# Layers 1 to 3 of a four-layer graph attention kernel: program order instead of a scheduler's order, earlier weight loads, later stores

## The chip, the cores and the metric

The kernel runs on one core of a Trainium2 chip. The metric is the device time of one execution in microseconds (us), lower is better. The kernel before takes 2342.57 us (median of three runs, 2339.33 to 2343.09).

## What is computed

Four graph attention layers in a row over 4096 nodes with 256 features each, all with the same adjacency matrix (about one entry in 256 set, and the diagonal). Each layer projects the features, makes a score for every pair of neighbours out of a term of the row and a term of the column, takes the softmax over the neighbours of a row, sums the neighbours' values with these weights, adds the layer's input and normalises the row. Cut to its core (h is the projection, a1 and a2 are the attention vectors):

```python
s1, s2 = h @ a1, h @ a2
e = leaky_relu(s1[:, None] + s2[None, :], 0.2)
e = where(adj > 0, e, -inf)
x = layernorm(x + softmax(e) @ h)
```

Layers 0 and 1 have four heads of 64 features, layer 2 two heads of 128 with biases. Layer 3 has one score, but two softmaxes (of e and of -e) over the unprojected x, a product with a matrix for both, and an ELU. All arithmetic is in float32.

## The kernel before

The adjacency matrix is sparse, so a row tile (128 rows) doesn't meet all 4096 columns. While layer 0 runs, `lists` packs the columns that each row tile needs into 13 groups of 128 column indices (`idx`) and a mask for each group (`maskC`). With the row tile's own 128 columns there are 14 positions, in two halves of seven.

**A row tile** (class `RowTile`). `load` brings the edge terms S (L619), the mask mk (L621), the tile's own value rows G (L626, "own-row load") and the input rows y (L925) through SyncE's queue, and 13 gathers of value rows by index through GpSimd (L629). `half` makes the weights of seven positions: in layers 1 and 2 ScalarE's exponentials L670 with VectorE's masked products L671, in layer 1 also VectorE's L666 and L667; in layer 3 ScalarE's L657, L658 and L660 with VectorE's L659 and L661. TensorE multiplies weights and values (L679 in layer 1, L682 in layers 2 and 3). In layer 1 ScalarE copies the sum out (L689) and TensorE transposes it back (L697). `finish` divides by the softmax's sum and adds y (L982, L983, L985; in layer 3 L967, L970 and L987 to L995), and `norm` normalises the row on VectorE: L935, L936, and then 15 operations on one number for each row (L944 to L954), among them three Newton steps for an inverse square root, each step of four operations that need one another's results, and L956, which writes y. L958 stores y.

**A projection** (class `Projection`) follows for each finished row tile of layers 0 to 2: transpose (L532), copy (L537 on ScalarE), product (L546, L549), row (L564 to L572, stored by L574), edge (L578, L584, stored by L585). Its results are what the next layer gathers.

**Whole rows** (`whole_rows`). In layer 2 the last twelve row tiles, in layer 3 the last four, are not gathered: four row tiles at a time meet all 32 column tiles in turn (`units`), with values loaded by L888, a mask by L886 and edge terms once for a block of four, ScalarE's L900 (in layer 3 L903 with L905 or L907), VectorE's L901 (L908) and TensorE's L911. `whole` advances the units between the halves of the gathered row tiles. When a block's last unit is done, `whole_rows` calls `finish` for its four rows, one after the other.

**Buffers.** S and mk have 4 buffers, w 10, G 16 slots (and 14 more for the second halves in layer 3), pw 8, vw 6, y 9.

**What sets the order.** The kernel is written as a software pipeline: `part` runs twice for each row tile m, loads what m and m+1 still lack, and then `half_alone` (layers 0, 1) or `half_with_whole` (layers 2, 3) issues one half with pieces of the projection and of the finish of m-1; `close` joins a layer to the next. But this order isn't the one on the engines. The framework's scheduler [...] puts each engine's instructions in the order of that plan. An engine runs its queue in that order, and so does SyncE with the loads and stores: an entry that waits holds what is behind it.

The weights of the next layer are made in row tile 2 by `weights`: loads of a few matrices and vectors, small products on TensorE (L270, L279) and their scaling (L258 to L262).

Of the kernel before, what the change touches and what calls it, by code (L numbers as in the profile page):

```python
# [37 lines left out]
F32 = mybir.dt.float32  # L38
# [12 lines left out]
P = 128  # L51
# [78 lines left out]
def to_tiles(ap):  # L130
    return ap.rearrange("(t p) f -> p t f", p=P)
# [55 lines left out]
class Program:  # L187
# [24 lines left out]

    def weights(self, n):

        nc, ins, H = self.nc, self.ins, HEADS[n]
        V = F if n < 3 else 2 * F
        wext = self.wpool.tile([P, KT, 2 * F + 4 * H4], F32, name="wext")
        ablks, nats, brow = [], [], None
        if n < 2:
            nc.sync.dma_start(out=wext[:, :, :F], in_=to_tiles(ins[f"W{n}T"]))  # L220
            for k, a in enumerate(("src", "dst")):
                ablk = self.small.tile([P, KT, H4], F32, name=f"ablk{k}")
                nc.vector.memset(ablk, 0.0)
                for h in range(H4):
                    r = slice((h % 2) * D4, (h % 2) * D4 + D4)
                    vec = ins["a0s" if k == 0 else "a0d"][h] if n == 0 else ins["a1"][h, k * D4:(k + 1) * D4]
                    load_vec(nc, ablk[r, h // 2, h:h + 1], vec)
                ablks.append(ablk)
                nats.append(ins[f"W{n}"])
        elif n == 2:  # L230
            nc.sync.dma_start(out=wext[:, :, :F], in_=to_tiles(ins["W23T"]))
            for k in range(2):
                ablk = self.small.tile([P, KT, 2], F32, name=f"ablk{k}")
                nc.vector.memset(ablk, 0.0)
                for h in range(2):
                    load_vec(nc, ablk[:, h, h:h + 1], ins["a2"][h, k * P:(k + 1) * P])
                ablks.append(ablk)
                nats.append(ins["W21" if k == 0 else "W22"])
            brow = self.small.tile([1, F + 3 * H], F32, name="brow")
            nc.sync.dma_start(out=brow[:, :F], in_=ins["b23"].rearrange("(o f) -> o f", o=1))  # L240
            ones = self.small.tile([1, P], F32, name="ones")
            nc.vector.memset(ones, 1.0)
            self.ones = ones
        else:
            fc = to_tiles(ins["fc3"])
            for k in range(2):
                nc.sync.dma_start(out=wext[:, :, k * F:(k + 1) * F], in_=fc[:, k * KT:(k + 1) * KT, :])
                ablk = self.small.tile([P, KT, 1], F32, name=f"ablk{k}")
                for q in range(KT):
                    load_vec(nc, ablk[:, q, 0:1], ins["a3"][(k * KT + q) * P:(k * KT + q + 1) * P])  # L250
                ablks.append(ablk)
                nats.append(ins["W3T"])

        T = TERMS[n]

        def scaled(dst, src, k):

            nc.vector.tensor_scalar(dst[:, k * T:(k + 1) * T], src, SLOPE, None, op0=ALU.mult)  # L258
            if k == 1:
                nc.vector.tensor_scalar(dst[:, 2 * T:3 * T], src, NEG_SLOPE, None, op0=ALU.mult)  # L260
                if n == 3:
                    nc.vector.tensor_scalar(dst[:, 3 * T:4 * T], src, -NEG_SLOPE, None, op0=ALU.mult)  # L262

        for k in range(2):
            nat = self.io.tile([P, KT, F], F32, name="nat")
            nc.sync.dma_start(out=nat, in_=to_tiles(nats[k]))
            for m in range(KT):
                pw = self.bank(self.banks)
                for q in range(KT):
                    nc.tensor.matmul(pw[:, :T], nat[:, q, m * P:(m + 1) * P], ablks[k][:, q, :],  # L270
                                     start=(q == 0), stop=(q == KT - 1))
                scaled(wext[:, m, V:], pw[:, :T], k)
            if n == 2:
                bcol = self.small.tile([P, KT], F32, name=f"bcol{k}")
                for q in range(KT):
                    load_vec(nc, bcol[:, q:q + 1], ins["b21" if k == 0 else "b22"][q * P:(q + 1) * P])
                pb = self.bank(self.banks)
                for q in range(KT):
                    nc.tensor.matmul(pb[:1, :T], bcol[:, q:q + 1], ablks[k][:, q, :],  # L279
                                     start=(q == 0), stop=(q == KT - 1))  # L280
                scaled(brow[:, V:], pb[:1, :T], k)
        return wext, brow


    def lists(self, ctx):
# [191 lines left out]

    def run(self):
        ins, nc = self.ins, self.nc
        w0 = self.weights(0)  # L480
        layer = Layer(self, 0)
        with ExitStack() as ctx:
            lists = self.lists(ctx)
            xs = []
            for q in range(NT // 2):
                slot = self.g0.tile([P, 2 * ROW[0]], F32, name="G")
                nc.sync.dma_start(out=slot[:, :2 * F].rearrange("p (t f) -> p t f", t=2),
                                  in_=to_tiles(ins["x"][2 * q * P:2 * (q + 1) * P, :]))
                xs += [slot[:, :F], slot[:, F:2 * F]]

            line = [Projection(self, 0, w0, x, m, (self.ptwo[0], self.ptwo[1], self.pfour))
                    for m, x in enumerate(xs)]
            turns, listed = NT + 5, 0
            for m in range(turns):
                while listed < BT + LEAD and listed * turns <= m * (BT + LEAD):
                    next(lists)
                    listed += 1
                for k, step in enumerate(Projection.STEPS):
                    if 0 <= m - k < NT:
                        step(line[m - k])  # L500

            for m in range(NT):
                layer.part(m, 0)
                if m + LEAD < NT:
                    next(lists)
                layer.part(m, 1)
            for _ in lists:
                pass
        self.g1 = self.pool("g1", 14)
        self.bk, self.vp, self.dp = self.pool("bk", 1), self.pool("vp", 6), self.pool("dp", 8)  # L510
        self.mwp = self.pool("mwp", 2)
        for n in (1, 2, 3):
            following = Layer(self, n)
            layer.close(following)
            following.steps()
            layer = following
        layer.close(None)


class Projection:  # L520
# [184 lines left out]
class Layer:  # L705
# [3 lines left out]
    def __init__(self, prog, n):  # L709
        self.prog, self.n, self.nc, self.shared = prog, n, prog.nc, prog.shared  # L710
        self.count = NT - WHOLE[n] * BT
        self.tiles = {}
        self.loaded = set()
        self.units = self.whole_rows()
        self.total = WHOLE[n] * NT * (1 if n < 3 else 2)
        self.used = 0
        self.nxt = self.middle = self.stored = None
        self.group = []
        self.ready = []
        self.step = 0  # L720


# [21 lines left out]
    def part(self, m, part):  # L744


        if part == 0:
            if m == 2 and self.n < 3:
                self.set_banks()
                self.nxt = self.prog.weights(self.n + 1)  # L750
            for q in (m, m + 1):
                for half in range(2):
                    self.load(q, half)
        if WHOLE[self.n]:
            self.half_with_whole(m, part)
        else:
            self.half_alone(m, part)
# [63 lines left out]
    def close(self, following):  # L821

        last = self.count - 1
        self.step += 2
        if self.stored is not None:
            self.stored.store()
        if self.middle is not None:
# [28 lines left out]
        for _, y, m in self.ready:  # L856
            self.set_banks()
            Projection(self.prog, self.n + 1, self.nxt, y, m).all()
        if following is not None:
            for m in (1, 2):  # L860
                following.load(m, 0)
            following.tile(1).half(0)
            following.load(3, 0)
# [64 lines left out]
    def norm(self, y, m):  # L928
# [25 lines left out]
            nc.vector.tensor_tensor(r, r, u, op=ALU.mult)  # L954
        for i, (y, m) in enumerate(self.group):
            nc.vector.tensor_scalar(y, y, mv[:, i, 0:1], r[:, i:i + 1], op0=ALU.subtract, op1=ALU.mult)  # L956
            dst = self.prog.out if self.n == 3 else self.shared["x"][self.n + 1]
            nc.sync.dma_start(out=dst[m * P:(m + 1) * P, :], in_=y)  # L958
            if self.n < 3:
                self.ready.append((self.step + 1, y, m))  # L960
        self.group = []

    def positive(self, acc, whole=False):
# [5 lines left out]
        z = pool.tile([P, F], F32, name="zw", bufs=BT) if whole else pool.tile([P, F], F32, name="z")  # L969
        nc.scalar.activation(z, acc[:, :D], AF.Copy, scale=rec)  # L970
        return z

    def finish(self, m, acc, y, z):
        n, nc, ep = self.n, self.nc, self.prog.ep
# [483 lines left out]
```

## Time and profile before

The span of the profiled run is 2346.8 us, with 49,828 instructions. The table has what the profile gives by layer; the layers are cut at the first gather of each, so each row holds the last matmuls of the layer before it.

| stretch (us) | layer | PE busy | DVE busy | ACT busy | POOL busy | clock of PE | GB/s |
|---|---|---|---|---|---|---|---|
| 0 to 812 | 0, and the lists | 690.0 | 714.2 | 657.5 | 534.0 | 0.95 | 228 |
| 812 to 1350 | 1 | 480.3 | 472.6 | 444.0 | 396.8 | 0.96 | 175 |
| 1350 to 1811 | 2 | 406.8 | 341.3 | 316.8 | 277.1 | 0.96 | 180 |
| 1811 to 2347 | 3 | 475.4 | 310.2 | 329.1 | 374.7 | 0.94 | 243 |

PE is TensorE, DVE is VectorE, ACT is ScalarE, POOL is GpSimd. Busy times are of the engine's own work; what a queue spends on waiting or issuing isn't in them. The chain of work that ended last, followed back from the last instruction, has 47% of the span on PE, 20% on DVE, 18% in DMA, 8% on ACT, 4% in issue and 3% on POOL. SyncE's queue, all layers together, waited longest ahead of the stores L958 for the normalised row: 226.8 us, 80 times.

### The profile page before, as it was taken

The page shows a single profiled execution, that of the slowest core. Times are in us where ns is not written, and L with a number is a line of the kernel's source. Part 1 is how long each engine was busy: PE and PEld are TensorE (multiplying, and loading weights), DVE is VectorE, ACT ScalarE, POOL GpSimd, SP SyncE. Part 2 cuts the span into 40 slices and gives each one's busy share as a digit, 9 for nine tenths or more (in the row PEclk, how much of TensorE's full clock was granted, in tenths as well). Part 3 has the DMA queues.
Part 4 walks back from the last instruction along what each step waited for, and adds up shares of the span by engine and source line. Part 5 has one row for each costly group of instructions (what it writes and reads, how often), then busy time and mean ns, then how long its engine had stood idle before and what let it go on. Part 6 is the DMA issues. An engine that isn't in the chain of part 4 may idle for free.

```text
span 2346.8 us, 49828 instructions
## 1 busy us (share of the span) xinstructions
PE 2052.4 (87%) x15689; PEld 1864.7 (79%) x15689; DVE 1838.1 (78%) x6100; ACT 1747.3 (74%) x5137; POOL 1582.6 (67%) x1596
## 2 busy tenths in 40 slices
PE   4878898989988769999999889889898799979996
PEld 3668788888888759988888879888887688868885
DVE  3889999999987759989899859876866365656567
ACT  4779898897787749988888859877663666666663
POOL 2127887777788757777777767755553677777773
PEclk7999999999999979999999989999999899989998
DMA  8889687775555556666666657666665788888883
GB/s 278 267 269 322 220 284 255 245 268 155 157 140 159 148 168 182 190 176 170 174 175 183 167 147 202 200 187 188 187 179 150 248 250 276 268 245 267 272 251 119
DMA packets 250325, 492.01 MB, mean 210 GB/s; under 512 B 44385, under 2 KB 156610, under 8 KB 249666
## 3 DMA queue, kind: packets, MB, share of 16 engines
q0 software_dynamic: 81536, 245.30, 37.1%
q1 hardware_dynamic: 168514, 243.42, 32.5%
q8 instruction: 126, 2.06, 0.4%
q14 instruction: 149, 1.22, 0.2%
HBM read 436.24 MB, written 52.31 MB: 208 GB/s over the span
## 4 chain that ended last, share of the span: by engine, by line
PE 47%; DVE 20%; DMA 18%; ACT 8%; issue 4%; POOL 3%; SPq 0%; ACTq 0%; DVEq 0%; POOLq 0%
PE bank L679 17%; PE bank L682 12%; DMA G<-vals,idx 12%; PE bank L911 7%; PE bank L546 5%; DVE w L671 5%; PE bank L436 4%; DMA G<-vals 3%; POOL G L629 3%; DVE w L666 3%; DVE w L667 3%; ACT w L670 3%; DVE oh L430 2%; DMA raw<-in_adjB_dram 2%; ACT pw L900 1%
## 5 line engine op out<-in xcount | busy, mean ns | idle before, releaser
L629 POOL DMA_INDIRECT G<-vals,idx x1456 | 1569.6, 1078 | 718.5 <-issue 188.1
L670 ACT ACTIVATE w<-S,G 128x128 f32<-128x128 f32 x3248 | 1009.6, 391 | 204.7 <-DMA G<-vals,idx 194.6
L679 PE MATMUL bank<-w,G 128*65 128x128 f32 x7168 | 846.8, 279 | 94.9 <-DVE w L667 65.0
L679 PEld LDWEIGHTS bank<-w,G 128*65 128x65 f32 x7168 | 810.4, 142 | 109.8 <-DVE w L667 84.5
L682 PE MATMUL bank<-G,w 128*128 128x257 f32 (+1 forms) x2688 | 499.4, 344 | 34.8 <-ACT z L970 11.5
L682 PEld LDWEIGHTS bank<-G,w 128*128 128x128 f32 x2688 | 439.2, 196 | 84.7 <-ACT z L970 13.9
L671 DVE SCALAR_TENSOR_TENSOR w<-w,mk 128x896 f32<-128x896 f32 x272 | 292.6, 1082 | 42.8 <-ACT w L670 42.1
L911 PE MATMUL bank<-vw,pw 128*128 128x129 f32 (+1 forms) x2048 | 304.8, 306 | 14.3 <-ACT zw L970 13.0
L911 PEld LDWEIGHTS bank<-vw,pw 128*128 128x128 f32 x2048 | 279.4, 195 | 32.0 <-ACT zw L970 13.4
L666 DVE TENSOR_SCALAR w<-S,G 128x128 f32<-128x128 f32 x896 | 238.7, 298 | 80.0 <-DMA G<-vals,idx 78.9
L657 ACT ACTIVATE w<-S,G 128x128 f32<-128x128 f32 x392 | 137.9, 389 | 146.6 <-DMA G<-vals 96.6
L546 PE MATMUL bank<-wext,xT 128*128 128x268 f32 (+3 forms) x640 | 188.3, 427 | 49.7 <-ACT xT L537 45.9
L430 DVE TENSOR_SCALAR oh<-iota,place 128x256 bf16<-128x256 f16 (+2 forms) x992 | 223.7, 298 | 8.3 <-PE bank L436 7.9
L671 DVE SCALAR_TENSOR_TENSOR w<-w,bank 128x896 f32<-128x896 f32 x192 | 206.0, 1078 | 8.9 <-ACT w L670 8.8
L436 PE MATMUL bank<-mk,oh 128*128 128x132 fp8e4 x2336 | 188.7, 228 | 15.7 <-DVE oh L430 8.7
L436 PEld LDWEIGHTS <-oh 128*128 128x128 bf16 x2336 | 147.3, 100 | 51.3 <-DVE oh L430 23.5
L546 PEld LDWEIGHTS bank<-wext,xT 128*128 128x128 f32 x640 | 122.0, 208 | 72.8 <-ACT xT L537 50.8
L908 DVE TENSOR_TENSOR pw<-pw,mw 128x512 f32<-128x512 f32 x64 | 43.9, 690 | 137.8 <-ACT pw L907 71.2
L901 DVE SCALAR_TENSOR_TENSOR pw<-pw,mw 128x512 f32<-128x512 f32 x192 | 127.8, 687 | 21.2 <-ACT pw L900 19.8
L373 ACT ACTIVATE mk<-raw 128x1024 uint8<-128x1024 int32 x128 | 131.5, 1063 | 16.9 <-DMA raw<-in_adjB_dram 16.5
L900 ACT ACTIVATE pw<-Sw,d 128x512 f32<-128x512 f32 x192 | 132.9, 708 | 3.4 <-PE bank L911 3.2
L443 ACT ACTIVATE cm<-bank 128x384 uint8<-128x384 f32 (+1 forms) x160 | 70.1, 451 | 60.4 <-PE bank L436 58.4
(131 smaller groups left out, 1710.5 us busy)
## 6 DMA issues: line engine op xcount, KB each, us to landing
raw<-in_adjB_dram SPq DMA_DIRECT2D x128, 512.0 KB
mk<-maskC SPq DMA_DIRECT2D x112, 224.0 KB
G<-vals,idx POOLq DMA_INDIRECT x1456
S<-edge SPq DMA_DIRECT2D x64, 256.0 KB
vw<-vals SPq DMA_DIRECT2D x96, 129.0 KB
xp<-y SPq DMA_DIRECT2D x96, 128.0 KB
y<-xp SPq DMA_DIRECT2D x96, 128.0 KB
mw<-maskW SPq DMA_DIRECT2D x20, 528.0 KB
```

Of the source, the lines that this page charges most:

```text
L430: nc.vector.tensor_scalar(oh[:, :n * P], iota[:, :n * P], self.place[:, it, j:j + 1], None, op0=ALU.is_equal)
L436: nc.tensor.matmul(accs[b][:, s * MC:(s + 1) * MC], oh[:, (k - a) * P:(k - a + 1) * P], mk[:, j, it, :].bitcast(FP8), start=touches[b][0] ...
L546: nc.tensor.matmul(pp[:, :c1 - c0], self.xT[:, k, :], wext[:, k, c0:c1], start=(k == 0), stop=(k == KT - 1 and brow is None))
L629: nc.gpsimd.indirect_dma_start(out=self.place(pos), out_offset=None, in_=sh["v"][n][:NODES[t], :], in_offset=bass.IndirectOffsetOnAxis(ap= ...
L657: nc.scalar.activation(w[0][:, k, :], S[:, 0, :], AF.Relu, bias=d(k, 0))
L666: nc.vector.tensor_scalar(w[h][:, k, :], S[:, h, :], d(k, h), LEAST, op0=ALU.mult, op1=ALU.max)
L670: nc.scalar.activation(w[h][:, k, :], S[:, h, :], AF.Exp, bias=d(k, h))
L671: nc.vector.scalar_tensor_tensor(w[h], w[h], LEAST, mh, op0=ALU.max, op1=ALU.mult)
L679: nc.tensor.matmul(accs[0][:Wd, h * P:(h + 1) * P], v, w[h][:, k, :], **how)
L682: nc.tensor.matmul(a, w[h][:, k, :], v, **how)
L900: nc.scalar.activation(p, S[:, h], AF.Exp, bias=d)
L911: nc.tensor.matmul(accs[it][:, c:c + Wd], p[:, it, :], v[:, c:c + Wd], start=(j == 0 and h == heads[0]), stop=(j == NT - 1), skip_group_ch ...
```

## The change

Three edits, which belong together.

- Layers 1 to 3 are built under `manual_schedule(engines=None)`: each engine's queue keeps the order in which the kernel issues its instructions. Layer 0 and the lists stay with the scheduler.
- `weights` becomes a generator of two steps. The loads are issued in row tile 1, the products and their scaling in row tile 2, as before.
- A finished row is not stored in `norm` but noted in `unsaved`, and `save` stores it at the start of the next half step, behind that step's loads. The queue of SyncE meets the store later, when the row should be ready.

The purpose is that a queue isn't held by an entry that is not ready while others are. With the order kept, it is the kernel's text that has to see to this.

```diff
     def weights(self, n):
...
+        loaded, bcols = [], []
         for k in range(2):
             nat = self.io.tile([P, KT, F], F32, name="nat")
             nc.sync.dma_start(out=nat, in_=to_tiles(nats[k]))
+            loaded.append(nat)
+            if n == 2:
...
+                bcols.append(bcol)
+        yield None
+        for k, nat in enumerate(loaded):
             for m in range(KT):
                 pw = self.bank(self.banks)
...
-        return wext, brow
+        yield wext, brow
...
-        for n in (1, 2, 3):
-            following = Layer(self, n)
-            layer.close(following)
-            following.steps()
-            layer = following
-        layer.close(None)
+        with self.tc.manual_schedule(engines=None):
+            for n in (1, 2, 3):
+                following = Layer(self, n)
+                layer.close(following)
+                following.steps()
+                layer = following
+            layer.close(None)
...
         if part == 0:
+            if m == 1 and self.n < 3:
+                self.coming = self.prog.weights(self.n + 1)
+                next(self.coming)
             if m == 2 and self.n < 3:
                 self.set_banks()
-                self.nxt = self.prog.weights(self.n + 1)
+                self.nxt = next(self.coming)
             for q in (m, m + 1):
                 for half in range(2):
                     self.load(q, half)
+        self.save()
...
     def close(self, following):
         last = self.count - 1
         self.step += 2
+        self.save()
...
             Projection(self.prog, self.n + 1, self.nxt, y, m).all()
+        self.save()
...
         for i, (y, m) in enumerate(self.group):
             nc.vector.tensor_scalar(y, y, mv[:, i, 0:1], r[:, i:i + 1], op0=ALU.subtract, op1=ALU.mult)
-            dst = self.prog.out if self.n == 3 else self.shared["x"][self.n + 1]
-            nc.sync.dma_start(out=dst[m * P:(m + 1) * P, :], in_=y)
+            self.unsaved.append((m, y))
...
+    def save(self):
+
+        dst = self.prog.out if self.n == 3 else self.shared["x"][self.n + 1]
+        for m, y in self.unsaved:
+            self.nc.sync.dma_start(out=dst[m * P:(m + 1) * P, :], in_=y)
+        self.unsaved = []
```

More of the change, by code (lines that the diff above doesn't have):

```diff
@@ L266, in weights @@
             nc.sync.dma_start(out=nat, in_=to_tiles(nats[k]))
+            loaded.append(nat)
+            if n == 2:
+                bcol = self.small.tile([P, KT], F32, name=f"bcol{k}")
+                for q in range(KT):
+                    load_vec(nc, bcol[:, q:q + 1], ins["b21" if k == 0 else "b22"][q * P:(q + 1) * P])
+                bcols.append(bcol)
+        yield None
+        for k, nat in enumerate(loaded):
             for m in range(KT):
@@ L273, in weights @@
             if n == 2:
-                bcol = self.small.tile([P, KT], F32, name=f"bcol{k}")
-                for q in range(KT):
-                    load_vec(nc, bcol[:, q:q + 1], ins["b21" if k == 0 else "b22"][q * P:(q + 1) * P])
                 pb = self.bank(self.banks)
                 for q in range(KT):
-                    nc.tensor.matmul(pb[:1, :T], bcol[:, q:q + 1], ablks[k][:, q, :],
+                    nc.tensor.matmul(pb[:1, :T], bcols[k][:, q:q + 1], ablks[k][:, q, :],
                                      start=(q == 0), stop=(q == KT - 1))
                 scaled(brow[:, V:], pb[:1, :T], k)
-        return wext, brow
+        yield wext, brow
     def lists(self, ctx):
@@ L479, in run @@
         ins, nc = self.ins, self.nc
-        w0 = self.weights(0)
+        _, w0 = self.weights(0)
         layer = Layer(self, 0)
@@ L718, in __init__ @@
         self.group = []
-        self.ready = []
+        self.ready, self.unsaved = [], []
         self.step = 0
```

## Prediction

> **What bounds the kernel now.** I read the busy time by stage first, then the idle time ahead of each engine in each stage, then the timelines. The four layers stand apart in the gathers (L629, 13 for each row tile): layer 0 until 812 us, layer 1 until 1350, layer 2 until about 1811, layer 3 to the end. Cut once more where the pace is even (columns: stretch, length, busy time of PE, PEld, DVE, ACT, POOL with counts, granted clock, DMA share, GB/s):
>
> ```profile
> 862.00:1350.00 488.00, 446.62 (x3748) 419.35 (x3749) 443.13 (x1409) 420.64 (x1407) 369.76 (x389) 0.97 0.64 175
> 1420.00:1780.00 360.00, 320.34 (x2557) 307.81 (x2555) 275.93 (x883) 268.43 (x729) 228.81 (x214) 0.97 0.67 189
> 1880.00:2300.00 420.00, 396.85 (x1790) 344.25 (x1788) 247.96 (x743) 269.44 (x578) 319.46 (x310) 0.97 0.85 261
> ```
>
> Layer 1 (first row) is paced by GpSimd's issue of gathers, although POOL shows only 370 of 488 us. Its timeline in that layer:
>
> ```profile
> 1051.76 0.95 POOL L629 DMA_INDIRECT G<-vals,idx  x1 [0.30 <-issue]
> 1053.01 0.95 POOL L629 DMA_INDIRECT G<-vals,idx  x1 [0.30 <-issue]
> 1054.26 0.95 POOL L629 DMA_INDIRECT G<-vals,idx  x1 [0.30 <-PE bank L679]
> ```
>
> One starts every 1.25 us, without a break: 13 x 1.25 = 16.3 us for a row tile (389 x 1.25 = 486 of the 488 us). DVE is right behind: 443 of 488.
>
> Layers 2 and 3 (second and third row) are paced by TensorE: 320 of 360 and 397 of 420 us. What little it waits for is named by its waits (time in total, times, longest), for 1420 to 1780 us and then for 1811 to the end:
>
> ```profile
> PE bank L546 <- ACT xT L537: 32.2, 14, 6.0
> ...
> PE bank L911 <- ACT zw L970: 13.0, 1, 13.0
> PE bank L682 <- ACT z L970: 11.5, 6, 3.7
> PE bank L682 <- issue: 8.7, 1, 8.7
> PE bank L682 <- DVE z L989: 6.5, 1, 6.5
> ```
>
> Behind the ACT entries of layer 3 stands the load of a row tile's own rows. ACT, in order, is held by it, and in SyncE's queue that load is held by the stores:
>
> ```profile
> ACT w L657 <- DMA G<-vals: 96.6, 20, 7.2
> SPq L958 <- DVE y L956: 80.4, 20, 13.0
> ```
>
> [...] VectorE in layer 1 with the normalisation's small operations between others, and at the end of the kernel with that chain alone:
>
> ```profile
> 1056.18 0.15 DVE L952 TENSOR_TENSOR u<-u,v 128x1 f32<-128x1 f32 x1
> 1056.25 0.28 DVE L666 TENSOR_SCALAR w<-S,G 128x128 f32<-128x128 f32 x1
> 1056.44 0.15 DVE L953 TENSOR_SCALAR u<-u 128x1 f32<-128x1 f32 x1
> ...
> 2338.36 0.16 DVE L952 TENSOR_TENSOR u<-u,v 128x1 f32<-128x1 f32 x1
> 2338.55 0.15 DVE L953 TENSOR_SCALAR u<-u 128x1 f32<-128x1 f32 x1
> 2338.74 0.16 DVE L954 TENSOR_TENSOR b<-b,u 128x1 f32<-128x1 f32 x1
> ```
>
> Between others, L952 takes 0.07 us from VectorE (1056.18 to 1056.25). In the bare chain each link takes 0.19 us. [...] PEld, 344 of 420 us in layer 3, is high as well, and the 28 matmuls of a half row tile follow each other at 0.217 us in the timeline, so I take TensorE as full there.
>
> **The change, part by part.** Nothing is added or removed; only order changes. I compared each engine's order in both programs.
>
> 1. *SyncE.* The own-row load now stands directly behind its mask load and ahead of the store, whose row was finished half a step before. What it then waits for is its slot, which the row tile two earlier gives up about one row tile (16 us) ahead of need. This removes the layer 3 waits: of the 13.0 us, about 3 stay (four evictions L970 of 0.47 us, with their reciprocals, still stand ahead of TensorE's next group), and the entries of up to 3.7 us go, 10.5 us in all. Gain 20 us.
>
> 2. *ScalarE.* In layer 2 the copy L537 now stands behind the 14 exponentials of its half and ahead of that half's whole-row work. TensorE does its 14 products meanwhile (28 passes x 0.11 = 3.1 us), so the copy is ready. The 32 us go; with 4 us of smaller waits gain 36 us.
>
> 3. *VectorE, layer 1.* The scheduler had dealt the normalisation out between L666, L667 and L671. Now a tile is 21 operations in one dependent chain: reciprocal 0.19, then L983, L985, L935 0.46 each, L936 0.22, 15 small ones x 0.19, L956 0.33: 5.0 us. The rest from start to start in the trace: L645 0.53, L666 14 x 0.196, the waits of L667 for them 2 x 0.115, L667 2 x 0.99, L671 6 x 1.0, rows (L566 to L572) 0.47: 11.95 us. Sum 16.95 us a row tile, against 16.3 for POOL. VectorE becomes the bound: 30 tiles x 0.65 = 20 us lost. ScalarE (42 x 0.29 + 1.0 = 13.3) and TensorE (about 15) fit inside.
>
> 4. *VectorE, ends of whole-row blocks.* Four rows finish together, and the order now has the four chains one behind the other, with no weight product between: 4 x 5.0 = 20 us in layer 2, three times; 4 x 6.0 = 24 us in layer 3, once (there L992, ScalarE's L993 and L995 lengthen it: 2214.5 to 2216.9 us for the part up to L936, the rest as above). They start only when TensorE has finished the block. What it has queued then: the first time a half row tile and a projection (3.1 + 4.2 us, but VectorE has another row's chain ahead, 6 us): idle about 19 us. The second time a unit of the new block, which needs VectorE's product first: 21. The third time L578, behind VectorE's row operations, which follow the chains: 21. Loss 61 us. In layer 3: 24 plus one product, 25 us, where the present kernel idles 8.7 us (gaps of 6.5 and 2.2 at 2301 to 2311): loss 17.
>
> 5. *Weights and the transitions between layers.* The scheduler already issued these loads early; the products L270 cost TensorE 0.9 us of waiting in layer 2. Cost nothing, hidden by the gathers of the row tile before. Between layers the last row's chain becomes 1 or 2 us shorter, since no other product is put ahead of it, and units that filled TensorE's wait come later. I take 0, between -10 and +10.
>
> Sum: -20 - 36 + 20 + 61 + 17 = +42 us. 2342.6 + 42 = 2385 us.
>
> The unknown is what other work costs in strict order. Bounds: layer 1 at 16.3 (VectorE's chain somehow absorbed, 20 us better) or at 18 us a tile (VectorE also waits for ScalarE within a half: 30 x 1.7 = 51, 31 us worse). I take 16.95, since ScalarE's order lets it start a half as soon as its gathers land.
>
> **The rivals.**
> - *The loads decide.* Item 1 and 2 come as worked out, and the chains hide: buffers of ten w and eight pw tiles let VectorE run ahead, and the four chains cost no more than now. 2342.6 - 56 = 2287 us. For it: 96.6 us of ScalarE's waits, and 18% of the span with DMA in the chain of waits. Against: a block's chains cannot start ahead of its last product, whatever the buffers.
> - *Losses and gains cancel.* The chains hide half (31 + 13 less 9 already there is 35), layer 1 loses 20: 2342.6 - 56 + 55 = 2342 us.
> - *Worse.* Layer 1 at 18 us a tile, the rest as forecast: 2385 + 31 = 2416 us.
>
> **How the numbers follow.** Forecast 0.54, worse 0.22, cancelled 0.10, loads decide 0.14. Faster by over 0.2%: 0.14 and a third of the cancelled case, 0.17. Within 0.2%: 0.05. Slower: 0.78. The range reaches over the cancelled case toward the loads' case and past the worse one with 10 us for the transitions: 2324 to 2428.
>
> **What would show it.** Right: in the timeline of layer 1, L951 to L954 in an unbroken chain at 0.19 us and gathers more than 1.25 us apart, VectorE above 95% there, 16.9 to 17.2 us a tile. TensorE idle three times for about 20 us in layer 2 and once for 25 in layer 3. ScalarE's wait for the own-row load below 20 us, TensorE's for L537 below 8. Wrong: gathers still every 1.25 us in layer 1, or no idle stretch of TensorE above 10 us at a block's end; then the chains are hidden, and the time falls below 2340.

## The result, and the profile after

The changed kernel takes 2500.68 us (median of 4 runs, 2496.67 to 2506.53); the kernel before, on the same chip, 2340.95. The ratio is 1.0685, 95% interval 1.066 to 1.071. The direction was forecast, the size was not: +160 us against +42, outside the range.

To see where the time went, I cut both profiled executions (spans 2346.8 and 2504.8 us) at first gathers of row tiles: row tile 4 of layer 1, and row tile 3 of layers 2 and 3. Every gather is in both traces, so the cuts lie at the same gathers; how far the whole rows are by then can differ. The "forecast" column is the prediction's sum, put where each item belongs.

| Part | Before | After | Difference | Forecast |
|---|---|---|---|---|
| A: layer 0, opening of layer 1 | 893.2 | 905.9 | +12.7 | 0 |
| B: layer 1, opening of layer 2 | 516.6 | 567.6 | +51.0 | +20 (item 3) |
| C: layer 2, opening of layer 3 | 460.1 | 545.4 | +85.3 | +25 (items 2 and 4) |
| D: layer 3, end | 476.8 | 485.9 | +9.1 | -3 (items 1 and 4) |

First the stretches of even pace in the kernel after, with the same columns as before: layer 1, layer 2, the opening of layer 3, layer 3.

```profile
906.00:1372.00 466.00, 401.19 (x3377) 374.85 (x3378) 442.42 (x1271) 364.91 (x1237) 333.24 (x351) 0.99 0.60 164
1473.00:1857.00 384.00, 324.48 (x2613) 313.38 (x2612) 298.97 (x842) 257.17 (x689) 218.84 (x208) 0.93 0.60 174
1857.00:2019.00 162.00, 83.50 (x393) 69.03 (x392) 66.54 (x232) 50.88 (x147) 50.83 (x53) 0.75 0.44 137
2019.00:2446.00 427.00, 398.12 (x1817) 345.61 (x1815) 280.12 (x831) 295.13 (x592) 331.11 (x312) 0.97 0.85 265
```

And the opening of layer 3 in the kernel before, cut at the same gathers:

```profile
1762.00:1870.00 108.00, 83.53 (x435) 70.87 (x434) 55.44 (x235) 51.16 (x123) 53.12 (x52) 0.89 0.66 197
```

The row of layer 1 holds 27 row tiles: 466 / 27 = 17.3 us each, where it was 16.3, and VectorE is busy 442 of 466 us. In the opening of layer 3 TensorE is busy for 83.5 us, as before, but of 162 us instead of 108, with 393 matmuls instead of 435 and at a clock of 0.75 instead of 0.89.

GpSimd's timeline in layer 1 now has a hole in each row tile. The last line starts 1.98 us after the one before it and was released by VectorE:

```profile
1159.26 0.95 POOL L637 DMA_INDIRECT G<-vals,idx  x1 [0.30 <-PE bank L687]
1160.51 0.95 POOL L637 DMA_INDIRECT G<-vals,idx  x1 [0.30 <-issue]
1162.49 0.94 POOL L637 DMA_INDIRECT G<-vals,idx  x1 [1.04 <-DVE u L967]
```

VectorE in layer 1 at that moment, in the chain of one row (L965 to L967 are L951 to L953 of before):

```profile
1160.39 0.16 DVE L965 TENSOR_TENSOR u<-b 128x1 f32<-128x1 f32 x1
1160.58 0.16 DVE L966 TENSOR_TENSOR u<-u,v 128x1 f32<-128x1 f32 x1
1160.78 0.15 DVE L967 TENSOR_SCALAR u<-u 128x1 f32<-128x1 f32 x1
```

A link each 0.19 to 0.20 us, with nothing between, as forecast. Now what TensorE waits for in part C (in all, times, longest):

```profile
PE bank L925 <- DVE pw L915: 57.8, 15, 22.2
PE bank L586 <- DVE row L580: 28.6, 10, 20.1
PE bank L690 <- DVE w L667: 26.0, 2, 16.1
PE bank L925 <- DMA vw<-vals: 13.0, 1, 13.0
...
PE bank L554 <- ACT xT L545: 2.0, 4, 0.5
```

The last line is the wait that item 2 was to remove. In the same part of the kernel before it was the longest of all:

```profile
PE bank L546 <- ACT xT L537: 33.2, 16, 6.0
```

The first two lines hold the three ends of blocks (21.4, 22.2 and 20.1 us). The third and fourth were not forecast: both lie in the opening of layer 3. And the waits of ScalarE and of SyncE's queue that stood behind item 1, from 1900 us to the end:

```profile
ACT w L665 <- DMA G<-vals,idx: 64.5, 65, 6.3
...
SPq L990 <- DVE y L970: 130.2, 23, 12.0
```

ScalarE no longer waits for the load of a row tile's own rows (`G<-vals`, without `idx`; 96.6 us before). What it waits for are gathers, and for these it waits longer than before (64.5 us; 49.8 before, from 1811 us to the end). The stores hold the queue longer too (130.2 against 80.4 us), yet in the even stretch of layer 3 no engine waits for a load of SyncE's queue.

### The profile page after: what moved, and what is told of

The parts are those of the page before. It is cut to its first block, busy times and chain, and to the rows that moved or that the text cites. A ratio compares the mean times of both kernels' runs of the same rounds, so it can differ in the third digit from the quotient of the medians.

```text
span 2504.8 us, 49774 instructions
## 1 busy us (share of the span) xinstructions
PE 2064.9 (82%) x15689; PEld 1871.5 (75%) x15689; DVE 1954.9 (78%) x6100; ACT 1757.1 (70%) x5137; POOL 1585.1 (63%) x1596
## 4 chain that ended last, share of the span: by engine, by line
PE 42%; DVE 31%; DMA 11%; ACT 7%; issue 7%; POOL 2%; SPq 1%; DVEq 0%; POOLq 0%; ACTq 0%
PE bank L690 14%; PE bank L687 13%; DVE w L679 7%; PE bank L925 7%; DMA G<-vals,idx 4%; DVE w L674 4%; ACT w L678 4%; PE bank L443 4%; PE bank L554 3%; DVE w L675 3%; DMA raw<-in_adjB_dram 2%; DVE oh L437 2%; DMA mk<-maskC 2%; POOL G L637 2%; DVE st L949 1%
## 5 line engine op out<-in xcount | busy, mean ns | idle before, releaser
L678 ACT ACTIVATE w<-S,G 128x128 f32<-128x128 f32 x3248 | 980.7, 391 | 50.9 <-DMA G<-vals,idx 30.9
L690 PE MATMUL bank<-G,w 128*128 128x257 f32 (+1 forms) x2688 | 503.7, 348 | 79.1 <-DVE w L667 52.6
L690 PEld LDWEIGHTS bank<-G,w 128*128 128x128 f32 x2688 | 445.2, 200 | 127.7 <-DVE w L667 54.5
L925 PE MATMUL bank<-vw,pw 128*128 128x129 f32 (+1 forms) x2048 | 311.8, 311 | 84.3 <-DVE pw L915 61.7
L674 DVE TENSOR_SCALAR w<-S,G 128x128 f32<-128x128 f32 x896 | 207.9, 301 | 44.9 <-DMA G<-vals,idx 44.8
L443 PE MATMUL bank<-mk,oh 128*128 128x132 fp8e4 x2336 | 189.2, 227 | 16.4 <-DVE oh L437 11.2
L679 DVE SCALAR_TENSOR_TENSOR w<-w,bank 128x896 f32<-128x896 f32 x192 | 197.3, 1080 | 2.4 <-ACT w L678 2.2
L554 PE MATMUL bank<-wext,xT 128*128 128x268 f32 (+3 forms) x640 | 176.7, 407 | 11.2 <-ACT xT L545 7.1
L665 ACT ACTIVATE w<-S,G 128x128 f32<-128x128 f32 x392 | 127.0, 389 | 69.7 <-DMA G<-vals,idx 64.5
L667 DVE TENSOR_TENSOR w<-w,mk 128x896 f32<-128x896 f32 x56 | 61.4, 1096 | 138.4 <-ACT w L666 138.0
L380 ACT ACTIVATE mk<-raw 128x1024 uint8<-128x1024 int32 x128 | 131.7, 1065 | 20.1 <-DMA raw<-in_adjB_dram 19.8
L572 ACT ACTIVATE row<-bank 128x4 f32<-128x4 f32 (+1 forms) x128 | 22.6, 177 | 174.9 <-PE bank L557 105.4
L915 DVE SCALAR_TENSOR_TENSOR pw<-pw,mw 128x512 f32<-128x512 f32 x192 | 120.8, 694 | 28.9 <-ACT pw L914 22.1
L914 ACT ACTIVATE pw<-Sw,d 128x512 f32<-128x512 f32 x192 | 121.6, 708 | 21.5 <-DMA Sw<-edge 16.5
```

Source lines behind the costliest of these rows:

```text
L380: nc.scalar.activation(mk[:, q:q + 2, :, :P], src, AF.Copy, scale=EDGE)
L443: nc.tensor.matmul(accs[b][:, s * MC:(s + 1) * MC], oh[:, (k - a) * P:(k - a + 1) * P], mk[:, j, it, :].bitcast(FP8), start=touches[b][0] ...
L554: nc.tensor.matmul(pp[:, :c1 - c0], self.xT[:, k, :], wext[:, k, c0:c1], start=(k == 0), stop=(k == KT - 1 and brow is None))
L665: nc.scalar.activation(w[0][:, k, :], S[:, 0, :], AF.Relu, bias=d(k, 0))
L674: nc.vector.tensor_scalar(w[h][:, k, :], S[:, h, :], d(k, h), LEAST, op0=ALU.mult, op1=ALU.max)
L678: nc.scalar.activation(w[h][:, k, :], S[:, h, :], AF.Exp, bias=d(k, h))
```

## The experiments

Two theories. **V**: the loss is VectorE's strict order, that is the unbroken chains in layer 1 and at the ends of blocks. **J**: the loss lies in the openings of the layers, where the kernel's own order is poor on all queues. In the table, A to D are the parts above, in us of the profiled execution; the ratio is to the kernel before on the same chip. Its median lay between 2341 and 2348 us on the chips of the table, so that differences of medians between rows are sure to a few us only. e13 and e14, at a lower clock, and e16, which repeats e7, are in the text.

| Run | A | B | C | D | Median us | Ratio (95%) |
|---|---|---|---|---|---|---|
| before | 893.2 | 516.6 | 460.1 | 476.8 | 2340.95 | 1 |
| after | 905.9 | 567.6 | 545.4 | 485.9 | 2500.68 | 1.0685 (1.066 to 1.071) |
| e1 | 901.6 | 525.3 | 476.3 | 469.4 | 2373.9 | 1.0115 (1.0066 to 1.0163) |
| e2 | 902.2 | 530.3 | 459.7 | 484.2 | 2379.17 | 1.0146 (1.0098 to 1.0194) |
| e3 | 889.1 | 555.7 | 529.9 | 484.5 | 2457.7 | 1.0473 (1.0425 to 1.0522) |
| e4 | 904.7 | 568.5 | 522.7 | 482.4 | 2475.03 | 1.0543 (1.0493 to 1.0594) |
| e5 | 894.5 | 516.1 | 463.0 | 471.8 | 2342.23 | 1.0001 (0.9981 to 1.0022) |
| e6 | 896.0 | 566.5 | 520.2 | 483.8 | 2468.83 | 1.0539 (1.0514 to 1.0565) |
| e7 | 895.5 | 512.3 | 457.7 | 468.5 | 2330.15 | 0.9942 (0.9919 to 0.9964) |
| e8 | 902.6 | 531.1 | 544.2 | 491.4 | 2464.13 | 1.0515 (1.0494 to 1.0537) |
| e9 | 895.9 | 635.6 | 521.8 | 509.2 | 2561.89 | 1.0934 (1.0896 to 1.0972) |
| e10 | 885.8 | 521.8 | 486.3 | 491.7 | 2386.58 | 1.0191 (1.0156 to 1.0225) |
| e11 | 897.3 | 515.3 | 460.8 | 470.1 | 2337.59 | 0.9968 (0.9955 to 0.9981) |
| e12 | 888.9 | 526.0 | 487.2 | 482.8 | 2384.77 | 1.0183 (1.0149 to 1.0217) |
| e15 | 891.6 | 519.6 | 453.1 | 467.4 | 2338.79 | 0.9962 (0.9948 to 0.9975) |

The parts are of one execution each. The kernel of e7, profiled a second time (e16), has 889.5, 513.6, 458.6 and 470.5 us: without any difference in the kernel A is 6 us apart, the others up to 2.

### e1: VectorE's order left to the scheduler

```diff
-        with self.tc.manual_schedule(engines=None):
+        E = mybir.EngineType
+        with self.tc.manual_schedule(engines={E.PE, E.Activation, E.Pool, E.SP}):
```

> The changed kernel, but VectorE's queue in layers 1 to 3 is left to the scheduler; the other four queues keep the kernel's order. Theory V (most of the 160 us is VectorE's order: unbroken chains, four rows' chains one behind the other): about 25 us of layer 1 and 70 to 80 us at the ends of blocks come back, 2395 to 2410 us, 16.3 us a row tile in layer 1, and no stretch of some 20 us without TensorE at a block's end. Theory J (most of it lies in the joins between layers, where loads, TensorE and ScalarE stand in the kernel's order): at most 40 us come back, 2460 us or more.

2373.9 us, below even what V expected: 127 us of the 160 go with VectorE's order. B and C fall by 42 and 69 us. The even stretch of layer 2 takes 331.8 us, less than in the kernel before (352.1), so the gain of item 2 is real once the chains don't cover it. C stays 16 us above before: J has a share.

### e2: only SyncE's order kept

```diff
+        with self.tc.manual_schedule(engines={E.SP}):
```

> The changed kernel, but only SyncE's queue keeps the kernel's order in layers 1 to 3; the scheduler orders the other engines. Theory V: SyncE's order is not what costs, and layer 3 gains its 20 us of waits for own rows: 2320 to 2345 us. Theory J, in the form that late loads of the next layer (edge terms, masks and values of whole rows) hold the joins: 2370 to 2400 us.

2379 us, 1.5% slower than before. That is J's range, but it doesn't show J's reason. The order of the loads alone, one of the things the change was for, gains nothing. In layer 3 ScalarE's wait for its own rows is gone, but in that stretch it now waits 101.9 us for gathers (26.8 before), and TensorE is busy 412 us of it against 400: work on the whole rows that the scheduler had put into the opening now lies inside layer 3. Most of the loss is elsewhere, 9 us in A and 14 in B, and was not followed up.

### e3: the next layer's first half row tile behind the last projections

```diff
     def close(self, following):
...
             self.tile(last).finish()
-            if following is not None:
-                following.tile(0).half(0)
...
             first.transpose()
-            following.tile(0).half(0)
             first.copy()
...
         self.save()
         if following is not None:
+            following.tile(0).half(0)
             for m in (1, 2):
```

> The changed kernel with one edit of close: the first half row tile of the next layer is issued behind the last projections of this layer instead of ahead of them. Theory V: the joins cost little, 2490 to 2500 us. Theory J: TensorE no longer waits for gathers with three projections queued behind that half, the wait of 16 us at the start of layer 3 goes, and all gathers that need every row come earlier: 2460 to 2475 us.

43 us come back, and they come from the openings: 17.4, 11.9 and 15.1 us in those of layers 1, 2 and 3. To see what stood there, take TensorE and then GpSimd in the opening of layer 3 in the changed kernel:

```profile
1937.51 0.27 PE L586 MATMUL bank<-ident,row 128*1 128x128 f32 x1 [0.94 <-DVE row L580]
1953.92 9.34 PE L690 MATMUL bank<-G,w 128*128 128x257 f32 x28 [16.14 <-DVE w L667]
1963.09 0.38 PE L540 MATMUL bank<-ident,y 128*128 128x128 f32 x2
...
1985.42 8.95 PE L690 MATMUL bank<-G,w 128*128 128x257 f32 x28 [9.89 <-DVE w L667]
```

```profile
1896.04 1.74 POOL L637 DMA_INDIRECT G<-vals,idx  x1 [0.30 <-issue]
1941.05 0.94 POOL L637 DMA_INDIRECT G<-vals,idx  x1 [43.27 <-issue]
```

The first gathers of layer 3 start at 1941, 43 us after the last of layer 2. The first half row tile (x28, L690) needs them, and it stands in TensorE's queue ahead of the remaining projections (L540), which need nothing of it. They sit behind it for 16 us, and the gathers of the next row tiles need their rows. With the half behind them, the waits of TensorE in this opening show it:

```profile
PE bank L690 <- DVE w L667: 4.7, 1, 4.7
```

4.7 us instead of 26.0. (The wait of 13.0 us for the first value rows became one of 12.5 us for the whole rows' weights.)

### e4: the four chains of a block spread, one row for each following half

```diff
-            for it, m in enumerate(tiles):
-                self.finish(m, accs[it], self.load_x(m), zs[it])
+            ys = [self.load_x(m) for m in tiles]
+            zz = [self.weighted(accs[it], zs[it]) for it in range(BT)]
+            for it, m in enumerate(tiles):
+                self.later.append((m, ys[it], zz[it]))
```

> The changed kernel, but at the end of a block of whole rows VectorE only takes the four sums out (reciprocal and product), and each row is added and normalised at the end of one of the next four halves. Theory V: three stretches of about 20 us without TensorE in layer 2 and one of 25 us in layer 3 shrink to 3 to 5 us each, 2425 to 2440 us. If TensorE's idle time there has another cause, or comes back elsewhere because layer 2 is not held by TensorE: 2480 us or more.

Neither expectation is met. The stretches of 20 us are gone (the longest in layer 2 is 10.5 us), but only 26 us come back. A chain of 5 us is still unbroken, and the whole rows' products behind it still come late: TensorE waits 28.4 us in all for them in part C, where it was 57.8. The idle time returned in smaller pieces.

### e5: the two small edits under the scheduler

```diff
-        with self.tc.manual_schedule(engines=None):
+        if True:
```

> The change without its kept order: weights loaded a row tile ahead and stores half a step later are in, but the scheduler orders every queue as before. Both theories (V: VectorE's strict order costs; J: the strict order between the layers costs) say that the two small edits are worth nothing by themselves: 2341 us, between 2335 and 2350. If instead the edits carry part of the loss (weights' loads or late stores colliding with others), it is above 2360.

No difference. Under the scheduler the early loads of the weights and the late stores cost and bring nothing: the loss comes with the kept order.

### e6: the openings left to the scheduler

```diff
             layer.close(following)
-            following.steps()
+            with self.tc.manual_schedule(engines=None):
+                following.steps()
```

> Order kept on all engines inside layers 1, 2 and 3 only; what closes one layer and opens the next is left to the scheduler. J says that the three transitions return to near those of the kernel before (101.9, 75.6, 108.0 us from the first gather of row tile 31 to that of the next layer's row tile 4, and so on; 106.6, 101.2, 161.6 in the changed kernel), so about 70 us of the 84 come back, less the 20 us of the block's end that lies in the last: 2500 - 65 = 2435 us, layers 1 to 3 unchanged at 17.27 us a row tile in layer 1. V says the transitions are long because of VectorE's chains at the end of the block, which stay: not below 2470.

Half of what J expected, 32 us, and 1 us below V's bound. The opening of layer 2 keeps 98.5 of its 101.2 us, that of layer 3 is at 140.4. To hand an opening to the scheduler is thus of little use in the opening of layer 2. What does shorten it is to move the half (e3, 11.9 us) and to deal out VectorE's chains in layer 1 (e8).

### e7: e1 and e3 together

> VectorE's order left to the scheduler, the other engines' kept, and the next layer's first half row tile moved behind the last projections of the closing layer, on TensorE, ScalarE and GpSimd. If the two effects add up (VectorE free: 2374 us; the moved half: 43 us less), it comes to 2331 us, a little below the kernel before. If the moved half only gave back what VectorE's order had lost at the same place, it stays at 2365 to 2374.

The two effects add: 2330 us, below the kernel before. The same kernel once more, beside e15:

> The kernel of e7 (VectorE free, half moved) again, on the same chip as e15, so that the two transitions can be compared: 2330 us again, with 128 us from layer 2 to 3.

It took 2329.97 us, ratio 0.9918 (0.9886 to 0.9949). So the kept order on the other four engines, together with the moved half row tile, is worth 12 to 18 us, if VectorE is left to the scheduler. What the moved half does under the scheduler alone was not measured. Its layer 2 and opening of layer 3:

```profile
1408.00:1738.00 330.00, 317.14 (x2627) 309.70 (x2626) 276.34 (x847) 257.65 (x690) 236.24 (x209) 0.98 0.70 204
1738.00:1865.00 127.00, 84.21 (x369) 68.04 (x368) 54.77 (x228) 49.30 (x143) 52.01 (x52) 0.76 0.56 172
```

Layer 2 is 22 us shorter than before, the opening 20 us longer, and C as a whole hardly moves.

### e8: the chain in layer 1 dealt out by hand

`norm` becomes a generator, and one of its operations follows each VectorE product of the next row tile; every queue keeps its order.

```diff
                     nc.vector.tensor_scalar(w[h][:, k, :], S[:, h, :], d(k, h), LEAST, op0=ALU.mult, op1=ALU.max)
+                    L.tick()
...
             nc.vector.tensor_tensor(u, r, r, op=ALU.mult)
+            yield
```

> All orders kept, but in layer 1 each row's small normalisation operations are dealt out by hand, one behind each product of the following row tile, in place of an unbroken chain. If a link costs 0.19 us only because it waits for the one before, and 0.07 us between others, VectorE loses 18 x 0.12 = 2.2 us a row tile and GpSimd paces again: 16.3 us a row tile against 17.27, 27 x 0.95 = 26 us less: 2475 us. If the pace of layer 1 has another cause (VectorE waiting for ScalarE's exponentials, buffers freed late), the row tile stays at 17 us or more and the time at 2495 to 2505.

The row tile takes 16.55 us on average, 16.3 to 16.4 after the first few, which is the pace of GpSimd again, and the kernel gains 36.5 us, 10 more than expected. VectorE's timeline in layer 1 (L973 and L975 are L965 and L966 of the kernel after):

```profile
1149.70 0.15 DVE L973 TENSOR_TENSOR u<-b 128x1 f32<-128x1 f32 x1
1149.77 0.28 DVE L674 TENSOR_SCALAR w<-S,G 128x128 f32<-128x128 f32 x1
1149.96 0.15 DVE L975 TENSOR_TENSOR u<-u,v 128x1 f32<-128x1 f32 x1
1150.03 0.27 DVE L674 TENSOR_SCALAR w<-S,G 128x128 f32<-128x128 f32 x1
```

The same link now takes 0.07 us of VectorE (1149.70 to 1149.77). The gain lies half in layer 1 (466.4 to 446.8 us) and half in the opening of layer 2 (101.2 to 84.3). From a row tile's first gather to its statistics on VectorE (L949; L935 before) it is 60 us in the middle of layer 1 of the changed kernel, 43 to 46 here, 40 to 42 before. While VectorE sets the pace, the gathers run ahead as far as the buffers allow, and this backlog is worked off after the last gather of the layer.

### e9: only VectorE's order kept

```diff
+        with self.tc.manual_schedule(engines={E.DVE}):
```

> Order kept on VectorE alone in layers 1 to 3, the other four queues left to the scheduler. If VectorE's order is by itself the larger part of the loss (with it free the kernel ran at 2374 us, 127 us less), the kernel is at 2440 to 2480 us, with 17.2 us a row tile in layer 1 and three idle stretches of TensorE of 20 us in layer 2. If the loss needs several orders together (VectorE's chains cost only because nothing else may be reordered round them on TensorE and ScalarE), it is at 2360 to 2410 us.

Neither: 2562 us, slower than with all orders kept, and 20.1 us a row tile in layer 1. ScalarE's waits in layer 1:

```profile
ACT aT L697 <- PE bank L687: 122.4, 26, 6.2
```

The scheduler puts ScalarE's copy L697 where it waits for TensorE; behind it the exponentials come late, and VectorE, in strict order, waits 58.9 us for them (none in the kernel after). So VectorE held to the kernel's order, while the others keep the scheduler's, is worse than either whole. This isn't so of every engine: with SyncE alone held, e2 lies between the two.

### e10 to e12: all orders kept and repaired; loads of the whole rows early

e10 is e3 with the chains of layers 1 and 2 dealt out, behind the whole rows' products (L915) too, and `y` with 12 buffers for 9.

> Order kept on every engine; the next layer's first half row tile stands behind the last projections, and the small normalisation operations of layers 1 and 2 are dealt out one to four behind each product (the four rows of a block too; layer 3 and the last rows of a layer as they were; y has 12 buffers in place of 9). V with J: dealing gives 36 us in layer 1 (as measured) and in layer 2 the two idle stretches of 20 us plus the pieces that spreading whole chains left (52 us against VectorE free), the moved half 43: 2501 - 36 - 50 - 43 = 2370 us. If a strict order on VectorE costs for another reason than the unbroken chains, layer 2 stays above 370 us and the kernel above 2400.

2386.6 us: 114 of the 160 us come back with every engine still in order. The even stretch of layer 2 takes 337.8 us, far from the 370 that would have spoken for another cost of VectorE's order than its unbroken chains. In part C, where the kernel after has waits of 57.8 us for L915, this one has 12.4 us in all, of which these are the largest:

```profile
PE bank L929 <- DVE u L979: 8.9, 1, 8.9
PE bank L929 <- DVE pw L918: 1.9, 2, 1.5
```

What is left to the kernel before is 26 us in C and 15 in D. The longest idle stretches of TensorE there come from the chains of layer 2's last block (16.7 us) and of layer 3's only block (25.0 us), which were not dealt out, and from the first value rows of the whole rows (12.8 us). The three more buffers of `y` were not tried apart from the rest.

e11 adds to e7 that the whole rows' first loads are issued ahead of the next row tiles' loads; e12 adds the same to e10.

```diff
             following.tile(0).half(0)
+            if WHOLE[following.n]:
+                next(following.units)
             for m in (1, 2):
```

> As the kernel with VectorE free and the moved half (2330 us), with the first loads of the whole rows of the next layer (their edge rows, masks and first four value rows) ahead of the loads of its row tiles 1 and 2. There TensorE idled 13.3 us for the first whole-row product at 1853 us. If that product waits for loads that stand too late in SyncE's queue, this idle goes in layer 3's opening (and part of the like in layer 2's): 2330 - 13 = 2317 us, range 2312 to 2325. If the wait is for values that are themselves late (the last projections), it stays at 2326 to 2335.

> Order kept on every engine, with all three repairs: chains dealt out, the half moved, the whole rows' first loads early. If the three causes together are the whole loss, it comes near the kernel with VectorE free and the same loads: 2317 to 2360 us. If VectorE's order carries a further cost, above 2380 us.

The early loads gain nothing in either: 2337.6 us where 2317 was hoped for, and 2384.8 us where e10 takes 2386.6, so that e12 is on the side of a further cost of VectorE's order, of which the chains that were not dealt out are a part. In e11 the idle stretch stays (13.8 us), only behind the whole rows' first product instead of ahead of it, and TensorE waits there for the weights of a half row tile. That everything in this opening waits for values which the last projections have only just written is a guess that no run shows.

### e13 to e15: the last opening once more

> VectorE free everywhere; TensorE, ScalarE, GpSimd and SyncE keep their order inside layers 1, 2 and 3 only, the transitions are the scheduler's. What is open is the transition from layer 2 to 3: 161.6 us in the changed kernel, 144.5 with VectorE free, 140.4 with the transitions scheduled, 108.0 in the kernel before. If the two shares (17 and 21 us) are separate and the rest comes of the order of the other engines in the transition, it is 108 to 125 us here, and the kernel at 2320 to 2345 us. If it stays at 135 to 145, the rest comes of the kept order in the first half row tiles of layer 3, and the kernel is at 2350 to 2370.

> As the one before, with the half row tile also written behind the last projections. Where the scheduler orders the transition by itself[...]: within 10 us of the kernel before this one. If the written order still decides, the transitions from layer 2 to 3 and from 0 to 1 are 15 us shorter each.

These two ran where TensorE's granted clock was 0.857 and the kernel before took 2888 us as well: 2922 and 2919 us, ratios 1.0118 (1.0083 to 1.0152) and 1.0096 (1.0061 to 1.0131). A row tile of layer 1 takes 23 us in both, and in e13 TensorE waits there for other engines for only 16 of 631 us, at a clock of 0.80, so they say nothing on the question. The first was run again:

> The kernel with VectorE free and the transitions left to the scheduler, once more, since the last call ran at a TensorE clock of 0.857, where the kernel before took 2888 us too. Expected as then: transition from layer 2 to 3 108 to 125 us and 2320 to 2345 us if the shares of VectorE and of the transition's own order are separate; 135 to 145 us and 2350 to 2370 if the kept order of layer 3's first half row tiles is the cause.

The opening takes 125.5 us, in e15 as in the repeated e7: at the edge of the two expectations, with 2339 us inside the first. The written order of the opening is not what keeps it above 108. But C as a whole (453 us) is shorter than before (460), since the even stretch of layer 2 gained more than the opening lost. The opening isn't longer for more work: the kernel before does 84 matmuls of layer 3's whole rows in it, e7 only 16. In e7 TensorE idles 43 us there instead of 24.5, and at a clock of 0.76 instead of 0.89 it is busy as long for fewer matmuls (84.2 us for 369, 83.5 us for 435). Nor are the 68 missing matmuls what makes it long: e2 has none of the 84 there, and its opening takes 109.9 us. So the cause of these 20 us stays open.

## Why the prediction was wrong

**Item 5 is the step that failed**: "Between layers the last row's chain becomes 1 or 2 us shorter ... and units that filled TensorE's wait come later. I take 0, between -10 and +10." I compared the order there without asking, for the first waiting instruction of each queue, what stood behind it. Instead of 0, the three openings grew by 4.7, 25.6 and 53.6 us, of which 20.1 are the end of the third block, which item 4 had priced: 64 us. The misplaced half (44 us in the three, e3) and the backlog that layer 1 leaves behind (17 us, e8) were in no item. The units did come later, as the item says, but e2 shows that this alone needn't lengthen the opening. By parts, the forecast missed 116 us:

- A, 12.7: 4.7 in the opening of layer 1, 8.0 in layer 0. e3 takes 17 out of the opening. Why layer 0 itself, whose order is the scheduler's, takes up to 11 us longer in most of these kernels stays open; two profiles of e7's kernel differ by 5 us there.
- B, 31: the opening of layer 2, forecast at 0, grew by 25.6: about 17 by the backlog (e8), 12 by the misplaced half (e3); in e10, with both repaired, it takes 75.8 us as against 75.6 before. The even stretch of layer 1 lost 25 us where item 3 had 20.
- C, 60: 30 us in the opening of layer 3 (26.0 for L667 and 13.0 for the first value rows, less 8.7 that were there before); 14 us of shorter waits for L915 (57.8 less 21.4 and 22.2), the "other work in strict order" that I had bounded for layer 1 only; 8 us more of TensorE's busy time (408.0 against 400.0) for about the same work (68 matmuls fewer of layer 3's whole rows, 81 more of layer 2's, which take 0.115 us each against 0.217, and 28 more of the row tiles); the rest is small waits and small differences of items 2 and 4. Some 20 us of this opening stay in e7, and some 24 in e10 beside its chains; their cause is open.
- D, 12: item 1 brought about 13 us instead of 20 (TensorE's waits in the even stretch fell from 24.3 to 11.1, with 9.5 us of new ones for the whole rows' products), and TensorE is busy 6 us longer (437.3 against 431.3), with the 68 matmuls that the kernel before had done in the opening.

**What held.** Item 3: VectorE became the bound of layer 1, with the chain at 0.19 us a link and 17.0 to 17.1 us a row tile in the even part (17.3 on average over the 27) against 16.95; only the backlog was left out of its sum. Its price was shown by itself in e8. (In that item 42 x 0.29 + 1.0 is 13.2 and not 13.3; nothing rests on it.) Item 4: idle stretches of 21.4, 22.2, 20.1 and 25.0 us against 19, 21, 21 and 25 (25 less 8.7 is 16, where the sum has 17). Item 2: the wait went from 33.2 to 2.0 us. Item 1: ScalarE's wait for its own rows went. The rivals failed: neither did the loads decide nor did the chains hide, and "worse" put its extra 31 us into layer 1, where they were not. That VectorE's order carries most of the loss (127 of 160) was right in kind, but e9 shows that it is not a property of that one queue.

A term that the prediction had none for is the clock. TensorE around the first end of a block in the changed kernel, in its timeline and by stretches:

```profile
1571.22 1.91 PE L554 MATMUL bank<-wext,xT 128*128 128x256 f32 x8
1594.54 5.59 PE L925 MATMUL bank<-vw,pw 128*128 128x129 f32 x32 [21.42 <-DVE pw L915]
...
1603.21 5.53 PE L925 MATMUL bank<-vw,pw 128*128 128x129 f32 x48
```

```profile
1580.00:1590.00 10.00, 0.00 (x0) 0.00 (x0) 8.61 (x43) 0.00 (x0) 0.01 (x1) 0.50 0.06 16
1600.00:1610.00 10.00, 10.00 (x92) 10.00 (x90) 6.33 (x10) 9.08 (x24) 4.73 (x5) 1.00 0.95 277
```

In the idle stretch the granted clock (third column from the end) is 0.50, and the first 32 matmuls after it take as long as 48 take later: 5.59 - 32 x 0.115 = 1.9 us on top of the 21.4 (0.115 is 5.53 / 48). While those 32 run, from 1594.54 to 1600.13 us, the clock averages 0.67; from 1600 to 1610 us it is 1.00. In the broken-up opening of layer 3 the clock averages 0.75, where it was 0.89.

## What to carry to other kernels

When a queue is to keep a written order, walk through the text at every boundary of a stage and ask of each instruction that will wait what stands behind it: here one half row tile ahead of the last projections cost 43 us in three places. Dependent chains of small operations have to be dealt out between independent ones in the text itself, since in this kernel a link costs 0.07 us there and 0.19 us alone; and a bound that moved to VectorE, a later engine, cost its backlog of 17 us once more at the end of the stage. Keep the order engine by engine and measure each set. Of those measured here, VectorE alone in order was the worst (2562 us) and all engines in order the next (2501). The fastest kernel left only VectorE to the scheduler and had the half row tile moved (2330 us; 2374 without the move, 2341 for the kernel before).

## What was not expected of the hardware

The three long waits of TensorE in layer 2 (21.4, 22.2 and 20.1 us) cost more than their length: the clock is 0.50 in each (1580 to 1590, 1720 to 1735 and 1870 to 1880 us in the changed kernel), and 1.8 to 1.9 us more went to slow matmuls after it (5.59 us for 32, 3.78 for 16 and 5.11 for 28, where the same take 3.7, 1.95 and 3.29 at a clock of 1.00). And the same kernels ran a quarter slower on one occasion at a granted clock of 0.857 (2888 us for the kernel before and 2922 for e13, against 2348 and 2339 beside e15), with 23 us a row tile in layer 1 in the two that were profiled: there the kernel with VectorE free and the openings scheduled was 1.2% slower than before, where it is 0.4% faster at 0.95.
